# A fused attention and feed-forward block on Trainium2: the rotary feature chain written back into PSUM, and the weight sums emitted one operation per slot

## The chip, the cores and the metric

The kernel runs on one core of one Trainium2 chip. What counts is the device time of one execution in microseconds. The core has five engines that the text names as the profile does: PE (TensorE, matrix products; PEld is its weight load), DVE (VectorE), ACT (ScalarE), POOL (GpSimd) and SP, whose queue issues all DMAs here. SBUF is the working memory; PSUM, eight banks of 128 partitions by 512 float32, receives matrix products.

## The reference

One sequence of 4096 tokens of width 512 passes through linear attention with 16 query heads and 4 key/value heads of 128, and then through a feed-forward block whose weights are surrounded by Hadamard transforms; each is followed by a residual sum and a layer norm. All is float32. Cut to the part that the change touches:

```python
q = q * cos + _rotate_half(q) * sin
k = k * cos + _rotate_half(k) * sin
qf = jax.nn.elu(q) + 1.0
kf = jax.nn.elu(k) + 1.0
def step(carry, inp):
    state, z = carry
    state = state + k_s[..., :, None] * v_s[..., None, :]
    z = z + k_s
    num = jnp.einsum('bhe,bhed->bhd', q_s, state)
    den = jnp.einsum('bhe,bhe->bh', q_s, z)[..., None] + EPS
    return ((state, z), num / den)
```

The feature is elu(x)+1, which the kernel computes as max(x+1, min(exp(x), 1)) with x+1 kept and exp taken with a bias of -1.

## The kernel before

Float32 precision comes from splitting each operand into a high part of the fast matrix type and a rest (`hilo`, L88 to L90: a copy on ACT at L89, a subtraction on DVE or POOL at L90), and from three products per pair.

The attention runs twice over 16 blocks of 256 tokens (n from 0 to 31), each time with half of the heads. One block has four slots (n, g, p), g a key/value head of the half, p a half of the block's four chunks of 64 tokens. The loop over the slots (L437) emits pieces of several generators, each `yield` being a place where the next piece of another one is put between. Per block there are four query projections (`proj_q`, five slots ahead of their use, QA = 5), one key projection (`proj_k`), one value projection (`proj_v`), the transposed keys (`nat_k`, L282), two states (`state`, L294), and in each slot scores (`scores`, L337 and L338, whose result is copied, corrected and masked at L344 to L351) and the numerators and denominators (`av`, L371 and L372).

Every projection has 24 matrix products into one PSUM bank of the pool pmm (L239, L191), which has three banks that rotate. For q and k the result `ps_qk` then goes through `rope`: ACT copies the two halves crosswise into the SBUF tile sw (L224, L225), POOL multiplies sw with the sine (L226), DVE multiplies ps_qk with the cosine in place (L227), DVE adds both and 1 into a new SBUF tile x1 (L230), ACT takes the exponential of x1 into sw (L231), DVE takes min and max (L234): for q into sw itself, for k into the feature tile kft. `proj_q` splits the feature afterwards: a copy into qh (L323) and the rest into ql (L325). The last reader of the PSUM bank is L230.

`wcomb(p)` (L385), for p from 0 to 7, makes sums of the feed-forward weights for later: it loads four tiles of 256 KB from wug, makes four sums on POOL (L394) and stores each by DMA. The tiles come from wres, the pool of 28 tiles that also holds the split attention weights. It is called whole in the slot (1,0) of the blocks n from 18 to 25 (L500). The second half of the attention weights is loaded from block 13 on, and the first reciprocals of denominators (`recip`) follow from block 17.

The order in which the instructions finally stand on each engine is made by the framework's scheduler: it keeps the dependences, estimates durations, and places each instruction by these and by the order of emission. Semaphores are set accordingly, and each engine runs its own order strictly.

After the attention come the output projection with the first layer norm (L724), the feed-forward's first product (L848) and its second (L971).

Of the kernel before, what the change touches and what calls it, by code (L numbers as in the profile page):

```python
# [9 lines left out]
F32 = mybir.dt.float32  # L10
F32R = mybir.dt.float32r
I32 = mybir.dt.int32
AF = mybir.ActivationFunctionType
ALU = mybir.AluOpType
# [29 lines left out]
def kernel(  # L44
# [6 lines left out]
    V, S, G, T = nc.vector, nc.scalar, nc.gpsimd, nc.tensor  # L51

    def dma(dst, src, pin=False):
        if dst.dtype == F32R:
            dst = dst.bitcast(F32)
        if src.dtype == F32R:
            src = src.bitcast(F32)
        i = nc.sync.dma_start(dst, src)  # L58
        if pin:
            tc.keep_in_program_order(i)  # L60

    cpool = ctx.enter_context(tc.tile_pool(name="cpool", bufs=1))
    wres = ctx.enter_context(tc.tile_pool(name="wres", bufs=28))
# [76 lines left out]
    with ExitStack() as es:  # L140
        early = ExitStack()
        pe = early.enter_context(tc.tile_pool(name="ae", bufs=2, side="right"))
# [11 lines left out]
        neg1 = p1.tile([128, 1], F32, name="neg1")  # L154
# [4 lines left out]
        def weights_v(s, j):  # L159
            W["v", s, j] = load_w(wv[s, :, j * 512:(j + 1) * 512])  # L160

        def weights_k(s, g):
            W["k", s, g] = load_w(wk[2 * s + g])

        def weights_q(s, g):
            for h in range(4):
                W["q", s, g, h] = load_w(wq[8 * s + 4 * g + h])
# [52 lines left out]
        def rope(ps, csb, f):  # L220
            cosb = csb[:, 0:1].to_broadcast([128, 2, 256])
            sinb = csb[:, 1:2].to_broadcast([128, 2, 256])
            sw = pe.tile([128, 2, 256], F32, tag="sw", name="sw", bufs=3)
            S.activation(sw[0:64], ps[64:128], AF.Copy)  # L224
            S.activation(sw[64:128], ps[0:64], AF.Copy)  # L225
            G.tensor_tensor(sw, sw, sinb, ALU.mult)  # L226
            V.tensor_tensor(ps, ps, cosb, ALU.mult)  # L227
            yield
            x1 = pe.tile([128, 2, 256], F32, tag="x1", name="x1", bufs=3)
            V.scalar_tensor_tensor(x1, ps, 1.0, sw, ALU.add, ALU.add)  # L230
            S.activation(sw, x1, AF.Exp, bias=neg1)  # L231
            yield
            f = sw if f is None else f
            V.scalar_tensor_tensor(f, sw, 1.0, x1, ALU.min, ALU.max)  # L234
            return f

        def proj(n, keys):
# [89 lines left out]
        def scores(j):  # L327
            n, g, p = slots[j]
            B = blk[n]
            qh, ql = B["q", g]  # L330
            pool, tag = (pmm, "mm") if j >= NQ - TAIL and j % 2 else (psc, "sc")
            ps = pool.tile([128, 2, 256], F32, tag=tag, name="ps_sc")
            for c2 in range(2):
                c = 2 * p + c2
                t = slice(64 * c, 64 * c + 64)
                khl = B["khl"][:, g, c]
                T.matmul(ps[:, c2], khl.rearrange("p l j -> p (l j)"), qh[:, :, t], start=True, stop=True)  # L337
                T.matmul(ps[0:64, c2], khl[:, 0], ql[:, :, t], start=False, stop=True,  # L338
                         skip_group_check=True)
            am = p2.tile([64, 512], F32, tag="am", name="am")  # L340
            A = p3.tile([128, 2, 256], F32R, tag="A", name="A", bufs=4)
            Af = A.rearrange("p a b -> p (a b)")
            psf = ps.rearrange("p a b -> p (a b)")
            S.activation(Af[0:64], psf[0:64], AF.Copy)  # L344
            B["A", g, p] = A
            yield
            V.tensor_tensor(am, psf[0:64], Af[0:64].bitcast(F32), ALU.subtract)  # L347
            V.tensor_tensor(Af[64:128], psf[64:128], am, ALU.add)
            for h in range(2):
                ah = Af[64 * h:64 * h + 64].rearrange("p (a q) -> p a q", q=64)  # L350
                G.affine_select(ah, ah.bitcast(F32), pattern=[[0, 8], [1, 64]], compare_op=ALU.is_ge,  # L351
                                fill=0.0, base=0, channel_multiplier=-1)
# [32 lines left out]
        def wcomb(p):  # L385
            r = {}
            for it in range(2):
                for kh in range(2):
                    x = wres.tile([128, 2, 2, 128], F32, tag="w", name="wq")
                    dma(x, wug[2 * p + it].rearrange("p (u k m) -> p u k m", u=2, k=4)[:, :, 2 * kh:2 * kh + 2])  # L390
                    r[it, kh] = x
            for key, o, a, b, op in (("S3", (0, 0), (0, 0), (1, 0), ALU.subtract), ("S1", (1, 0), (1, 0), (1, 1), ALU.add),
                                     ("S2", (1, 1), (0, 0), (1, 1), ALU.subtract), ("S4", (0, 1), (0, 1), (1, 1), ALU.add)):
                G.tensor_tensor(r[o], r[a], r[b], op)  # L394
                dma(was_d[p][key], r[o].rearrange("p u k m -> p (u k m)"))

        N = 2 * NB
# [14 lines left out]
        def go(gen):  # L412
            if gen is not None:
                next(gen, None)

        def run(gen):
            for _ in gen:
                pass
# [14 lines left out]
        for j in range(SA):  # L433
            run(scores(j))
        nsc = SA
        gk = gs1 = gv = None
        for i, (n, g, p) in enumerate(slots):  # L437
            nxt = n + 1 < N
            sl = (g, p)
            r = i - 4 * (NB - 1)  # L440
            if r == -6:
                for j in range(2):
                    weights_v(1, j)
                    weights_k(1, j)
            if r == 1 - QA:
                weights_q(1, 0)
            if r == 3 - QA:
                weights_q(1, 1)
            if i == NQ - 10:
                load_wo(NH - 2)  # L450
            if i == NQ - 3:
                early.close()
                late["s"] = ExitStack()
                late["p"] = late["s"].enter_context(tc.tile_pool(name="cl", bufs=2, side="right", reuse_waits="tile"))
                pre(0)
            go(gq)
            if sl == (0, 1):
                go(gk)
            if sl == (1, 0):
                go(gk)  # L460
            gq2 = proj_q(i + QA) if i + QA < NQ else None
            go(gq2)
            if sl == (0, 0):
                gk = proj_k(n + 1) if nxt else None
                go(gk)
                go(gs1)
                gs2 = state(n, 1)
                go(gs2)
            elif sl == (0, 1):
                gv = proj_v(n + 1) if nxt else None  # L470
                go(gv)
                go(gk)
                if n + 2 < N:
                    run(load_x(n + 2))
            elif sl == (1, 0):
                if nxt:
                    nat_k(n + 1)
            else:
                gs1 = state(n + 1, 0) if nxt else None
                go(gs1)  # L480
            go(gq)
            gsc = []
            while nsc < NQ and nsc <= i + SA + (i >= NQ - TAIL) + (i > NQ - TAIL):
                gsc.append(scores(nsc))
                go(gsc[-1])
                nsc += 1
            go(gq)
            if sl == (0, 0):
                go(gs2)
            elif sl == (0, 1):  # L490
                go(gv)
            elif sl == (1, 1):
                go(gs1)
            av(n, g, p)
            if sl == (0, 0):
                go(gs2)
            for x in gsc:
                go(x)
            gq = gq2
            if sl == (1, 0) and 18 <= n < 26:  # L500
                wcomb(n - 18)
            if sl == (1, 1):
                if NB + LAG <= n < N - 2 + LAG:
                    recip(n - NB - LAG)
                blk.pop(n - 1, None)
# [15 lines left out]
    def xtile(shape, dt, name):  # L521
        return mid.tile(list(shape), dt, tag="x4", name=name, bufs=2)
# [101 lines left out]
    with ExitStack() as es:  # L624
# [19 lines left out]
        for h in (NH - 2, NH - 1):  # L644
            w = xtile([128, 2, 512], F32R, "wx")
# [68 lines left out]
        for t in range(32):  # L714
            if t + 2 < 32:
                pre(t + 2)
            ps = pwo.tile([128, DM], F32, tag="wo", name="ps_wo")
# [35 lines left out]
            if t >= 29 and t < 31:  # L753
                x = late["p"].tile([128, 16, 128], F32, tag="nt", name="araw0", bufs=2)
                x = x.rearrange("p (s u k) m -> p s u k m", s=4, u=2)
# [41 lines left out]
    with ExitStack() as es:  # L797
# [23 lines left out]
        for n in range(NS):  # L821
            f, p = divmod(n, 8)
# [14 lines left out]
            for s, tag in enumerate(SEQ):  # L837
# [3 lines left out]
                for u in (1, 0):  # L841
                    if first:
                        bank[tag, u] = pgu.tile([128, 512], F32, tag=tag, name="ps_" + tag, bufs=4 if tag == "a" else 2)
                    ps = bank[tag, u]
# [8 lines left out]
                    if s in (0, 2, 4):  # L853
                        x = pa.tile([128, 512], F32, tag="sv", name="sv", bufs=6)
                        S.activation(x, ps, AF.Copy, scale=sc)  # L855
                        sv[s, u] = x
                    if s in (1, 4, 6):
                        src, k, q = {1: (ps, 0, 0), 4: (bank.get(("b", u)), 4, 3), 6: (ps, 2, 1)}[s]
                        x = utile("cc")
                        V.scalar_tensor_tensor(x, src, sc, sv[k, u], ALU.mult, ALU.add)  # L860
                        emit(u, q, x)
                    if s == 5:
                        if u == 1:
                            x = utile("sg")
                            S.activation(x, ps, AF.Silu, scale=sc)
                            c["g", 2] = x
                        else:
                            x = c.pop(("g", 2))
# [44 lines left out]
    with ExitStack() as es:  # L913
# [34 lines left out]
        for idx, (n, s) in enumerate(order):  # L948
# [10 lines left out]
            tag = SEQ[s]  # L959
# [3 lines left out]
            ps = bank[n, tag]  # L963
# [86 lines left out]
```

## Time and profile before

| what | us |
|---|---|
| three timed runs: median | 2352.28 |
| three timed runs: lowest and highest | 2348.13, 2353.02 |
| the profiled execution | 2347.88 |
| its span, first to last instruction | 2345.7 |
| busy PE, PEld | 2270.4, 2014.8 |
| busy DVE, ACT, POOL | 1808.5, 1403.3, 1244.4 |

The span of the profiled execution is the sum over all stages; the attention takes the first 966 us of it. Busy time on PE counts modelled ends of pipelined matrix products, so a full PE shows no holes, but isn't shown to be at its peak. In the groups of instructions the last columns say how long the engine idled just before them and what ended the idleness. A wait is put down to the semaphore that came last. The granted clock of PE was 0.988 of full speed over the span.

### The profile page before, as it was taken

How to read it: one execution, taken by the hardware profiler on the slowest of the kernel's cores; microseconds unless marked ns; L12 is line 12 of the kernel's file. 1: busy time of each engine (PE TensorE's matmuls, PEld its weight loads, DVE VectorE, ACT ScalarE, POOL GpSimd, SP SyncE). 2: the span in 40 equal slices, each digit the busy share in tenths (PEclk: the TensorE clock that was granted, in tenths of full speed). 3: DMA queues.
4: the chain of work that ended last, by engine and by line, in shares of the span. 5: the costliest groups of instructions: out<-in, count | busy, mean ns of one | idle time of the engine just before them, and what ended most of it. 6: DMA issues, size and time to landing. Idle time of an engine off the chain costs nothing.

```text
span 2345.7 us, 42356 instructions
## 1 busy us (share of the span) xinstructions
PE 2270.4 (97%) x14432; PEld 2014.8 (86%) x14432; DVE 1808.5 (77%) x2799; ACT 1403.3 (60%) x2482; POOL 1244.4 (53%) x1000
## 2 busy tenths in 40 slices
PE   7999999998999999799999999999999999899998
PEld 6999999988899999688878777788878888799998
DVE  6999999988798889778898676686776766765554
ACT  5777777766677777444444466655655655555553
POOL 2454544576654445367888526565565556633332
PEclk9999999999999999899999999999999999999999
DMA  6454555677744444878997977786666766877673
GB/s 185 145 147 147 157 159 151 177 213 219 209 133 133 129 132 139 276 253 266 283 294 257 303 238 217 237 256 188 226 208 189 243 189 198 278 238 249 224 253 117
DMA packets 369528, 484.16 MB, mean 206 GB/s; under 512 B 68670, under 2 KB 224384, under 8 KB 365344
## 3 DMA queue, kind: packets, MB, share of 16 engines
q1 hardware_dynamic: 369312, 481.45, 66.4%
q8 instruction: 114, 1.87, 0.3%
q14 instruction: 102, 0.84, 0.1%
HBM read 282.76 MB, written 156.76 MB: 187 GB/s over the span
## 4 chain that ended last, share of the span: by engine, by line
PE 78%; DVE 8%; DMA 6%; issue 4%; POOL 2%; ACT 2%; SPq 1%; DVEq 0%; ACTq 0%; POOLq 0%
PE ps_a L848 14%; PE ps_qk L244 13%; PE ps_wo L724 12%; PE ps_da L971 8%; PE ps_b L848 7%; PE ps_num L371 5%; PE ps_db L971 4%; PE ps_c L848 3%; PE ps_s L294 3%; PE ps_v L197 3%; PE ps_dc L971 2%; PE ps_sc L337 1%; PE ps_den L372 1%; PE ps_sc L338 1%; SPq L58 1%
## 5 line engine op out<-in xcount | busy, mean ns | idle before, releaser
L351 POOL TENSOR_SCALAR_AFFINE_SELECT A<-A 64x512 fp32r<-64x512 f32 x256 | 219.1, 856 | 289.5 <-DVE am L347 185.7
L244 PE MATMUL ps_qk<-xh,wh 128*128 128x256 f32 x1280 | 359.8, 281 | 7.6 <-ACT wh L89 3.9
L244 PE MATMUL ps_qk<-xh,wl 128*128 128x256 f32 x1280 | 358.1, 280 | 0.0
L244 PE MATMUL ps_qk<-xl,wh 128*128 128x256 f32 x1280 | 358.0, 280 | 0.0
L90 DVE TENSOR_TENSOR wol<-A,woh 128x512 fp32r<-128x512 f32 x217 | 229.1, 1060 | 112.4 <-ACT woh L89 94.6
L830 POOL TENSOR_TENSOR cc<-cc 128x512 f32<-128x512 f32 x96 | 148.7, 1550 | 286.1 <-ACT cc L827 137.2
L226 POOL TENSOR_TENSOR sw<-sw,csb 128x512 f32<-128x512 f32 x160 | 219.9, 1375 | 143.3 <-ACT sw L225 135.2
L244 PEld LDWEIGHTS ps_qk<-xh,wh 128*128 128x128 f32 x1280 | 243.5, 190 | 9.2 <-ACT wh L89 4.1
L244 PEld LDWEIGHTS ps_qk<-xl,wh 128*128 128x128 f32 x1280 | 242.9, 190 | 1.3
L244 PEld LDWEIGHTS ps_qk<-xh,wl 128*128 128x128 f32 x1280 | 242.9, 190 | 0.8
L89 ACT ACTIVATE hah<-hraw 128x512 fp32r<-128x512 f32 x224 | 139.8, 630 | 133.5 <-PE ps_da L971 64.3
L89 ACT ACTIVATE woh<-A 128x512 fp32r<-128x512 f32 x217 | 135.6, 630 | 131.1 <-PE ps_b L848 74.9
L90 POOL TENSOR_TENSOR hal<-hraw,hah 128x512 fp32r<-128x512 f32 x80 | 105.8, 1324 | 189.9 <-PE ps_da L971 66.1
L848 PE MATMUL ps_a<-yoh,woh 128*128 128x512 f32 x512 | 202.4, 397 | 1.8 <-ACT sv L855 1.4
L848 PE MATMUL ps_a<-yol,woh 128*128 128x512 f32 x512 | 202.5, 396 | 0.0
L848 PE MATMUL ps_a<-yoh,wol 128*128 128x512 f32 x512 | 199.3, 396 | 0.0
L90 DVE TENSOR_TENSOR hal<-hraw,hah 128x512 fp32r<-128x512 f32 x144 | 106.2, 746 | 117.0 <-PE ps_da L971 41.8
L724 PE MATMUL ps_wo<-wh,oh 128*128 128x512 f32 x448 | 178.6, 399 | 4.6 <-ACT oh L89 4.6
L724 PE MATMUL ps_wo<-wh,ol 128*128 128x512 f32 x448 | 178.3, 398 | 0.0
L724 PE MATMUL ps_wo<-wl,oh 128*128 128x512 f32 x448 | 177.9, 397 | 0.0
L231 ACT ACTIVATE sw<-x,neg 128x512 f32<-128x512 f32 x160 | 115.5, 722 | 79.9 <-DVE x L230 78.0
L855 ACT ACTIVATE sv<-ps_a,wsc 128x512 f32<-128x512 f32 x192 | 127.1, 679 | 40.0 <-PE ps_a L848 39.9
(215 smaller groups left out, 7273.8 us busy)
## 6 DMA issues: line engine op xcount, KB each, us to landing
hraw<-hop_d SPq DMA_DIRECT2D x224, 256.0 KB
vd<-vhl SPq DMA_DIRECT2D x128, 256.0 KB
num_d<-num SPq DMA_DIRECT2D x128, 256.0 KB
rb<-rec_d SPq DMA_DIRECT2D x128, 256.0 KB
hop_d<-hS SPq DMA_DIRECT2D x128, 256.0 KB
nt<-num_d SPq DMA_DIRECT2D x31, 1024.0 KB
A<-in_wug_dram SPq DMA_DIRECT2D x93, 256.0 KB
hop_d<-cc SPq DMA_DIRECT2D x64, 256.0 KB
```

Source lines behind the costliest of these rows:

```text
L89: S.activation(hi, src, AF.Copy)
L90: eng.tensor_tensor(lo, src, hi.bitcast(F32), ALU.subtract)
L226: G.tensor_tensor(sw, sw, sinb, ALU.mult)
L231: S.activation(sw, x1, AF.Exp, bias=neg1)
L244: T.matmul(ps[:, j], W[key][wa][:, k * 128:(k + 1) * 128], B[xa][:, k], start=i == 0, stop=i == 11)
L351: G.affine_select(ah, ah.bitcast(F32), pattern=[[0, 8], [1, 64]], compare_op=ALU.is_ge, fill=0.0, base=0, channel_multiplier=-1)
L371: T.matmul(ps[:, c2], l, r, start=i == 0, stop=i == len(ops) - 1)
L724: T.matmul(ps, l[:, h], r, start=i == 0, stop=i == 47)
L830: G.tensor_tensor(x, x, c.pop(("g", q)), ALU.mult)
L848: T.matmul(ps, w[:, u, k], y[:, k], start=first and i == 0, stop=i == 5, skip_group_check=not first)
L855: S.activation(x, ps, AF.Copy, scale=sc)
L971: T.matmul(ps[:, j], ops[qd][al][:, r, js], BW[s][bl][ip], start=first and i == 0, stop=i >= 45, skip_group_check=True)
```

## The change

Two edits, both in the attention.

In `rope` the tile x1 is gone. The sum of L230 is written into ps_qk in place, the exponential reads ps_qk, and the minimum and maximum for q are written into ps_qk, too, in place of sw; for k they go into kft as before. `proj_q` is not edited, but its feature f is now the PSUM tile, so the copy into qh and the subtraction into ql read PSUM. So the bank is held until ql is made (q) or until kft is written (k).

`wcomb` becomes a generator that yields after its four loads and after each sum (the store of a sum is emitted at the next step), and `wcomb_all` runs the eight of them one after another. One step is emitted per slot in the blocks 17 to 27: 44 steps, of which 41 have work. The tiles get another name; pool and tag stay.

```diff
-            x1 = pe.tile([128, 2, 256], F32, tag="x1", name="x1", bufs=3)
-            V.scalar_tensor_tensor(x1, ps, 1.0, sw, ALU.add, ALU.add)
-            S.activation(sw, x1, AF.Exp, bias=neg1)
-            yield
-            f = sw if f is None else f
-            V.scalar_tensor_tensor(f, sw, 1.0, x1, ALU.min, ALU.max)
+            V.scalar_tensor_tensor(ps, ps, 1.0, sw, ALU.add, ALU.add)
+            S.activation(sw, ps, AF.Exp, bias=neg1)
+            yield
+            f = ps if f is None else f
+            V.scalar_tensor_tensor(f, sw, 1.0, ps, ALU.min, ALU.max)
             return f
@@
-                    x = wres.tile([128, 2, 2, 128], F32, tag="w", name="wq")
+                    x = wres.tile([128, 2, 2, 128], F32, tag="w", name="wsum")
                     dma(x, wug[2 * p + it].rearrange("p (u k m) -> p u k m", u=2, k=4)[:, :, 2 * kh:2 * kh + 2])
                     r[it, kh] = x
+            yield
             for key, o, a, b, op in (("S3", (0, 0), (0, 0), (1, 0), ALU.subtract), ("S1", (1, 0), (1, 0), (1, 1), ALU.add),
                                      ("S2", (1, 1), (0, 0), (1, 1), ALU.subtract), ("S4", (0, 1), (0, 1), (1, 1), ALU.add)):
                 G.tensor_tensor(r[o], r[a], r[b], op)
+                yield
                 dma(was_d[p][key], r[o].rearrange("p u k m -> p (u k m)"))
@@
+        def wcomb_all():
+            for p in range(8):
+                yield from wcomb(p)
+
+        gw = wcomb_all()
@@
-            if sl == (1, 0) and 18 <= n < 26:
-                wcomb(n - 18)
+            if 17 <= n < 28:
+                go(gw)
```

## The prediction

> **What bounds the kernel now.** I read the busy table, then the busy time by stage, then the chain of waits inside each stage, then the groups of the chain that the change edits, then the waits of the one stage in which TensorE is not full. The edited code runs only in the attention stage, about 0 to 966 us. By stage (length, then busy time of PE, PEld, DVE, ACT, POOL, then granted clock):
>
> ```profile
> 60.00:400.00 340.00, 339.90 (x2770) 324.14 (x2770) 315.63 (x521) 258.30 (x464) 169.12 (x156) 1.00 0.52 151
> 400.00:700.00 300.00, 279.32 (x2182) 261.81 (x2180) 259.91 (x417) 200.62 (x358) 180.34 (x161) 0.98 0.66 191
> 700.00:930.00 230.00, 230.00 (x1876) 219.50 (x1876) 202.12 (x346) 170.72 (x301) 110.77 (x110) 1.00 0.47 131
> 930.00:980.00 50.00, 36.06 (x211) 29.99 (x210) 37.42 (x60) 25.87 (x49) 21.50 (x24) 0.83 0.75 226
> ```
>
> In 60 to 400 and 700 to 930, 570 us, TensorE has no hole. A busy PE need not be at its peak, so I looked at matmul starts: 0.114 us apart in L244, almost without exception, and the same run of 38 matmuls recurs at 723.73, 751.67, 779.61 us, so a token block takes 27.94 us. The chain in those windows is nearly all PE. VectorE, 88 to 93% busy, is second and not on the end. The holes are elsewhere: in 0 to 60 (weights arriving, then VectorE), in 400 to 700 (second weight half, weight sums, first reciprocals) and in the drain after 930. Adding what each matmul start is late against its usual spacing, PE loses about 30 us in 400 to 660, 25 of them in 18 gaps over 0.5 us.
>
> The groups that the change edits (count | busy us, mean ns | idle before):
>
> ```profile
> L325 DVE TENSOR_TENSOR ql<-sw,qh 128x512 fp32r<-128x512 f32 x128 | 126.3, 987 | 6.8 <-ACT qh L323 5.6
> L231 ACT ACTIVATE sw<-x,neg 128x512 f32<-128x512 f32 x160 | 115.5, 722 | 79.9 <-DVE x L230 78.0
> L227 DVE TENSOR_TENSOR ps_qk<-ps_qk,csb 128x512 f32<-128x512 f32 x160 | 110.9, 693 | 25.6 <-ACT sw L225 24.2
> L230 DVE SCALAR_TENSOR_TENSOR x<-ps_qk,sw 128x512 f32<-128x512 f32 x160 | 108.6, 679 | 29.8 <-POOL sw L226 29.4
> L234 DVE SCALAR_TENSOR_TENSOR sw<-sw,x 128x512 f32<-128x512 f32 x128 | 92.4, 722 | 3.3 <-ACT sw L231 2.2
> L234 DVE SCALAR_TENSOR_TENSOR kft<-sw,x 128x512 f32<-128x512 f32 x32 | 30.8, 963 | 0.4 <-ACT sw L231 0.4
> ```
>
> L227 and L230, with one input in PSUM, hold 672 to 700 and 669 to 693 ns over all 160; L325 and L234, with both inputs in SBUF, spread to 2069 and 2405 ns. The waits of 440 to 700 us (total, times, longest):
>
> ```profile
> POOL wq L394 <- DMA wq<-in_wug_dram: 15.2, 7, 5.0
> PEld ps_num L371 <- POOL A L351: 13.2, 12, 3.4
> PE ps_num L371 <- POOL A L351: 10.5, 9, 3.2
> POOL wq L394 <- issue: 8.3, 2, 5.2
> PE ps_sc L337 <- DVE A L348: 6.1, 5, 2.2
> PEld ps_qk L244 <- DVE x L230: 2.5, 2, 1.6
> ```
>
> A weight sum whose load is late blocks POOL, the mask (L351) behind it is late, and PE waits for it. A projection waits for its bank (last row) almost never.
>
> **What the Trainium skill says.** "SBUF — State Buffer", section "Who interferes with whom": a VectorE instruction with at most one SBUF input doesn't contend with GpSimd, one with two contends with GpSimd reads. The spreads above agree. "PSUM — Partial Sum Buffer", section "Specifications (TRN2)": VectorE may take one tensor input from PSUM, GpSimd none. The new operations keep to it, and POOL's multiply L226 stays as it is. "Perfetto Trace Analysis", section "Optimization Strategy": equal bubbles on the engine that should be full can mean too few buffers; before, those two windows show none. No page prices a bank held longer.
>
> **The change, part by part.**
>
> *Faster VectorE operations.* Both inputs in SBUF become one. Taking 690 ns (L227's and L230's level): L325 128 x (987-690) = 38.0 us; L234 into the feature tile 128 x (722-690) = 4.1; L234 into kft 32 x (963-690) = 8.7; L230 now writes PSUM, as L227 does: 160 x (693-679) = +2.2. Together -48.6 us of VectorE. ScalarE reads PSUM in L231 and L323: copies from PSUM take 588 (L201), from SBUF 631 ns (L323), so -43 ns x 288 = -12 us. In the 570 us with PE full this is hidden behind PE and worth nothing. In 400 to 700 the pieces of the chain add up to some 81 us DVE, 53 DMA, 28 issue, 25 POOL, the rest mostly PE. VectorE's saving there is about a third of 48.6, 16 of 260 us or 6%, so 81 x 6% = 5 us. POOL, less disturbed (L226 means 1434 ns there, 1301 in the quiet window): 6% of 25, 1.5 us. Fill, where 21 of 30 us to 60 are DVE on the chain: 6%, 1.5 us with rounding. Drain: 0. ACT: 0. Sum -8; bounds 0 (DMA decides anyway) and -20 (most holes of the 30 us close, since a VectorE that is less loaded catches up sooner).
>
> *The bank is held longer.* The three banks of pmm rotate: projection j+3 takes the bank of j. Now the last reader is L230; after it is the subtraction into ql (for k the write of kft). Following each tile through the trace by the built order: from first matmul to the end of L230 9.5 us mean in 60 to 400 (8.2 in 700 to 925), to the end of L325 14.3 (13.5). The third next projection starts 14.0 us after a tile on average (two of them are one block: 27.94). Before, 4.5 to 5.8 us are spare. After, the built order keeps tiles more together (26.7 matmuls from a tile's first to last, formerly 30.3: -0.4 us), and VectorE work from L227 to ql falls from 7.9 to 7.4 us (-0.5), so the hold is about 12.6 to 13.4 and the spare 0.6 to 1.4.
>
> The tightest link in the built order is the q tile before k, whose bank the v projection takes. Ahead of its ql VectorE has k's add, sl and A. From k's last matmul: swaps 1.24, POOL 1.44, add 0.72, sl 0.68, A 0.71, ql 0.70, with waits between about 5.6 to 6.2 us. PE meanwhile has 24 matmuls of 0.114, some 26 of 0.118 and three state ones, 6.3 us. So it just fits, with no cover left: where it doesn't, each missing 0.1 us costs 0.1 us in each of some 20 quiet blocks. I take 0 there, bounds 0 and +8 (0.4 us a block). In 400 to 700 the hold to L325 is 17.5 us in the mean while blocks take about 32 (16 for three tiles): minus 1.4 as above, nothing is spare, and a late POOL operation now delays the bank as well as the mask. Much of that overlaps with waits that PE has anyway: +2, bounds 0 and +16. Behind a waiting projection stand the next scores and numerators in PE's queue, which restart POOL and VectorE: so a missed bank echoes once round. Fill: +1 for the same reason (five q tiles are projected ahead), bounds 0 and +5.
>
> *Weight sums one per slot.* Same 32 sums of 1.26 to 1.75 us, same 32 loads and 32 stores on SP, emitted from block 17 to 27. But the scheduler puts an operation where it thinks the operands are ready: sums stand in the built POOL order behind 82, 83, 84, 84, 85, 85, 85, 86 rope multiplies, formerly 82, 83, 84, 84, 85, 85, 86, 86, and the last behind 105 in both. Freed weight tiles pace them, not the new yields. So the 25 us that POOL idles before L394 mostly stay; another draw of places: -2, bounds -8 and +6. On SP a store that waits for its sum is queued ahead of later loads, as before.
>
> *Freed tile x1*: three SBUF buffers, used by nothing else.
>
> *Sum*: -8 + 0 + 2 + 1 - 2 = -7 us. The profiled execution took 2347.9 us (span 2345.7 and 2.2 around), so 2341 on its own scale. The three timed runs have median 2352.28, 4.4 above it; against these 2345.
>
> **Rivals.** *A, as summed*, 2345, own range 2337 to 2350. *B, the banks decide*: PE waits for a bank in each block, 0.4 x 20 = 8 us, and in 400 to 700 the bank turns POOL's delays into PE holes, +16; fill +5; against -8 and half of -2: +20, 2372; a milder form at half these prices +6, 2358. It decides once the mean hold passes 14.0 us. For it: a spare near 1 us and the link that just fits; in the built order 147 projection rows wait for VectorE alone, formerly 46. Against: a wait in the order isn't a wait in time, and the tiles' own chain, some 9.5 us without queues, leaves 4.5 us for queueing. *C, nothing moves*: PE is full where the operations got cheaper, DMA decides in the holes, the scheduler undoes the spreading: 2352. For it: 570 of 966 us. *D, the holes close*: VectorE and POOL recover before PE notices, 20 of the 30 us gone and 5 of the fill: 2327. For it: L348, L325 and L234 recur on the chain after each DMA delay. Against: 53 us of DMA on the chain are untouched.
>
> **How the numbers follow.** Chances: A 0.42, B 0.34, C 0.13, D 0.11. A measurement here can tell about 0.2%, 4.7 us, from no change. A lies mostly beyond it: 0.36 of 0.42; with D faster gets 0.47. Same: 0.06 of A, C's 0.10, some of mild B: 0.19. Slower: 0.34. The likeliest is 2345. The range takes D nearly whole and B to its full price less a little: 2324 to 2370.
>
> **What would show it.** Right: L324 and L233 at about 690 ns without spread, VectorE some 49 us less busy, PE as full in 60 to 400 and 700 to 930 with a 27.94 us block, fewer PE waits for A in 400 to 700. Wrong through B: waits of ps_qk and ps_v for VectorE's ql in each block, a block over 28.2 us, a lower granted clock. Wrong through D: PE's holes after 400 halved. If the sums alone matter, POOL's waits for wsum loads vanish while the bank waits stay nil.

## The result, and the profile after

The change made the kernel no faster: 2351.39 us after it (median of 12 runs, 2347.04 to 2354.41) beside 2347.94 before it on the same chip (median of 12, 2344.77 to 2353.02), a ratio of 1.0009 with a 95% interval of 1.0001 to 1.0017. The forecast was a gain of 7 us. The profiled execution after the change took 2354.41 us with a span of 2352.5, that of before 2347.88 with 2345.7. The former is the slowest of its twelve runs, 3 us above their median, so the stages below overstate the difference by about that much.

The edited operations did what was foreseen for them. The groups of instructions after the change (count | busy us, mean ns | idle time before, and what ended it):

```profile
L324 DVE TENSOR_TENSOR ql<-ps_qk,qh 128x512 fp32r<-128x512 f32 x128 | 88.0, 687 | 18.5 <-ACT qh L322 16.6
L233 DVE SCALAR_TENSOR_TENSOR ps_qk<-sw,ps_qk 128x512 f32<-128x512 f32 x128 | 88.1, 688 | 2.5 <-ACT sw L230 1.1
L233 DVE SCALAR_TENSOR_TENSOR kft<-sw,ps_qk 128x512 f32<-128x512 f32 x32 | 21.7, 678 | 0.2
L230 ACT ACTIVATE sw<-ps_qk,neg 128x512 f32<-128x512 f32 x160 | 109.9, 687 | 56.1 <-DVE ps_qk L229 54.7
L226 POOL TENSOR_TENSOR sw<-sw,csb 128x512 f32<-128x512 f32 x160 | 209.0, 1307 | 187.6 <-ACT sw L225 174.0 <-POOL A L350 8.7 <-issue 1.3
L350 POOL TENSOR_SCALAR_AFFINE_SELECT A<-A 64x512 fp32r<-64x512 f32 x256 | 197.9, 773 | 282.2 <-DVE am L346 179.9 <-DVE A L347 97.7 <-PE ps_qk L243 0.7
```

The two groups of GpSimd before it, the multiply and the causal mask:

```profile
L226 POOL TENSOR_TENSOR sw<-sw,csb 128x512 f32<-128x512 f32 x160 | 219.9, 1375 | 143.3 <-ACT sw L225 135.2 <-POOL A L351 1.5 <-DVE A L348 0.8
L351 POOL TENSOR_SCALAR_AFFINE_SELECT A<-A 64x512 fp32r<-64x512 f32 x256 | 219.1, 856 | 289.5 <-DVE am L347 185.7 <-DVE A L348 69.3 <-DVE khl L272 26.0
```

The rest ql fell from 987 to 687 ns, the key's minimum and maximum from 963 to 678, and GpSimd's multiply and mask, which nobody edited, from 1375 to 1307 and from 856 to 773. VectorE's idle time before ql rose from 6.8 to 18.5 us: it finished earlier and waited more. The same stages as before (length, then busy PE, PEld, DVE, ACT, POOL, then granted clock):

```profile
60.00:400.00 340.00, 340.00 (x2761) 322.69 (x2760) 303.17 (x519) 253.61 (x462) 150.34 (x156) 1.00 0.54 151
400.00:700.00 300.00, 280.01 (x2153) 262.04 (x2153) 239.66 (x409) 195.70 (x354) 161.98 (x159) 0.96 0.63 186
700.00:930.00 230.00, 228.54 (x1840) 214.74 (x1838) 188.03 (x340) 160.87 (x293) 105.91 (x107) 1.00 0.49 132
```

Read the counts of matmuls, not the busy time: with more or less full PE there are 2761 in place of 2770 in 60 to 400, 2153 in place of 2182 in 400 to 700, and 1840 in place of 1876 in 700 to 930. PE does less in each of these stretches although VectorE is freer in each. (The stretches are fixed, so a kernel that starts its blocks later also shows fewer matmuls.) The granted clock of PE in 400 to 700 us, the last column but two, is 0.96 after the change, 0.98 before. The waits of the two full stages, one fence for each (60 to 400, then 700 to 930; total, times, longest), show a line that before was not there:

```profile
PEld ps_v L197 <- DVE ql L324: 2.3, 11, 0.2
```

```profile
PEld ps_sc L336 <- DVE A L347: 2.5, 6, 0.5
PEld ps_v L197 <- DVE ql L324: 1.9, 8, 0.2
```

Eleven and eight times, about once in each block, the value projection waits for the bank that ql releases. In the fill a query projection waits 4.9 us for ql. So the bank is felt. The waits put down to ql are small, but they aren't all that PE stands still: the second full stage has 2.5 us for the correction A of the scores beside them.

A sharper measure is the start of each block's key transposes, which every kernel has 32 times. In us:

| kernel | block 2 starts | 2 to 12 | 12 to 22 | 22 to 30 |
|---|---|---|---|---|
| before | 94.3 | 278.7 | 312.8 | 223.5 |
| after | 98.1 | 281.2 | 316.5 | 227.8 |

After the change 3.8 us are lost in the fill, 2.5 in the first full stage, 3.7 in the stage with the weight work, 4.3 in the second full stage. In the two full stages the listed waits have the size of the loss: 2.3 us in the first, and 2.5 and 1.9 in the second. The drain gives 6.4 of these 14.2 back: the output projection starts at 978.8 in place of 971.0.

### The profile page after: what moved, and what is told of

It reads as the page before. It is cut to its first block, busy times and chain, and to the rows that moved or that the text cites. A ratio compares the mean times of both kernels' runs of the same rounds, so it can differ in the third digit from the quotient of the medians.

```text
span 2352.5 us, 42271 instructions
## 1 busy us (share of the span) xinstructions
PE 2280.3 (97%) x14432; PEld 2018.4 (86%) x14432; DVE 1768.2 (75%) x2799; ACT 1390.4 (59%) x2482; POOL 1208.7 (51%) x1000
## 4 chain that ended last, share of the span: by engine, by line
PE 79%; DMA 8%; DVE 6%; POOL 2%; issue 2%; ACT 2%; SPq 1%; ACTq 0%; DVEq 0%; POOLq 0%
PE ps_wo L731 14%; PE ps_a L855 13%; PE ps_qk L243 13%; PE ps_da L978 8%; PE ps_b L855 7%; PE ps_num L370 5%; PE ps_db L978 4%; PE ps_v L197 3%; PE ps_c L855 3%; PE ps_s L293 3%; PE ps_dc L978 2%; PE ps_sc L336 1%; DMA den_d<-ds 1%; DMA wsum<-in_wug_dram 1%; PE ps_den L371 1%
## 5 line engine op out<-in xcount | busy, mean ns | idle before, releaser
L350 POOL TENSOR_SCALAR_AFFINE_SELECT A<-A 64x512 fp32r<-64x512 f32 x256 | 197.9, 773 | 282.2 <-DVE am L346 179.9
L226 POOL TENSOR_TENSOR sw<-sw,csb 128x512 f32<-128x512 f32 x160 | 209.0, 1307 | 187.6 <-ACT sw L225 174.0
L230 ACT ACTIVATE sw<-ps_qk,neg 128x512 f32<-128x512 f32 x160 | 109.9, 687 | 56.1 <-DVE ps_qk L229 54.7
```

The lines of the kernel that those rows point to most:

```text
L230: S.activation(sw, ps, AF.Exp, bias=neg1)
```

## The experiments

All were timed in five rounds against the kernel before on the same chip. The brackets behind a ratio hold its 95% interval. Differences in us are of medians. The cuts of code leave out unchanged lines.

### Each edit alone

The first kernel has the feature chain in PSUM and the weight sums as before, the second the sums one per slot and the chain as before: each is one of the two edits of the diff shown above.

> Only the feature chain in PSUM; the weight sums as before. Holding theory (the v projection waits for the bank that the q tile before k keeps until ql): the quiet blocks 2 to 12 last 28.1 to 28.2 us as in the changed kernel, formerly 27.87, PEld of ps_v waits for ql in most of them, and the time is that of the changed kernel within 3 us (0 to 6 above before). Sums theory (the sums' new places cost, holding is free): blocks of 27.9 us and a time 4 to 8 us below before. Redraw theory (any edit shifts the schedule by a few us): blocks either way, time anywhere within 6 us.

> Only the weight sums one operation per slot; x1 in SBUF as before. Holding theory: quiet blocks 27.9 us, no bank wait, time within 3 us of before. Sums theory: 3 to 6 us above before, the loss between blocks 15 and 21. Redraw theory: up to 6 us either way between blocks 15 and 21 and nothing elsewhere.

The chain alone took 2353.60 us, ratio 1.0026 (1.0018 to 1.0035), the sums alone 2347.75, ratio 1.0002 (0.9994 to 1.0010). With the sums alone the blocks are as before except from 16 to 21, which shift by up to 3 us each way. So the sums alone are worth nothing that can be measured, and the loss belongs to the chain. With it come the 4.96 us gap between two matmuls of PE in the fill and the 19 waits of the value projection in the full stages. On top of the chain the sums may be worth something: the change with both edits has the ratio 1.0009 (1.0001 to 1.0017), the chain alone 1.0026, some 4 us more, with intervals that don't overlap. The profiled executions, 2354.41 and 2353.54 us, don't show where.

### The bank held longer, the operations as before

```diff
+        late1 = p1.tile([128, 1], F32, name="late1")
@@
             V.tensor_tensor(ql, f, qh.bitcast(F32), ALU.subtract)
+            V.tensor_tensor(late1, ps[:, 0, 0:1], ql[:, 0, 0:1].bitcast(F32), ALU.add)
```

> The kernel before, with one added element operation on VectorE behind each ql that reads ps_qk, so that the bank is held as long as in the change, without the cheaper VectorE operations (128 added operations of about 0.1 us, 13 us of VectorE). Holding theory: the hold is 14.3 us where the third next tile starts 14.0 after, so the bank is short in every block: 0.5 to 2 us a block, 15 to 45 us in all. If holding is free: 0 to 5 us.

2352.92 us, ratio 1.0025 (1.0016 to 1.0035): 6 us, far less than expected. The fill loses 3.9 us up to block 2, and the full stages have blocks of 28.05 and 28.11 us although no wait for a bank is seen there. The reads add 128 x 152 ns = 19.5 us to VectorE, so even these 6 us aren't the bank's alone. Taken by itself this run says that the hold is cheap. With VectorE's operations still slow it is; the last pair of experiments shows that with quick ones it isn't.

### The order of the key's and a query's projection

The bank that the value projection takes is that of the query projected ahead of the key. If the key is projected first, it takes the key's, which is free earlier.

```diff
+            if sl == (0, 0):
+                gk = proj_k(n + 1) if nxt else None
+                go(gk)
             gq2 = proj_q(i + QA) if i + QA < NQ else None
             go(gq2)
             if sl == (0, 0):
-                gk = proj_k(n + 1) if nxt else None
-                go(gk)
                 go(gs1)
```

> The changed kernel with the k projection of a block emitted ahead of the q projection of the slot (0,0), so that v takes the bank of k, which is free when kft is written, and not of the q tile before k. Holding theory: the wait of ps_v for ql goes, quiet blocks fall from 28.13 to 27.9 us, the time is 5 to 9 us below the changed kernel, 2 to 6 below before. If the block is longer for another reason (PE rows in another order, DMA): blocks stay at 28.1 us and the time within 3 us of the changed kernel.

> The kernel before with k emitted ahead of q, the control of e4. There no projection waits for its bank, so holding theory says nothing is gained: time within 2 us of before. If e4's gain comes from the order alone, this gains 3 to 7 us too.

On top of the change: 2345.94 us, ratio 0.9998 (0.9990 to 1.0006). The value projection's waits for ql are gone (three for the key's kft stand in their place, 1.6 us in all) and the full blocks take 28.0 and 27.9 us in the mean, in place of 28.1 and 28.5. In the kernel before the same order leaves them at 27.9 to 28.0 us, so it isn't the order by itself that shortens them: that link was the cause of the longer blocks. The other expectation fell: in the kernel before, where no such wait exists, the same order gained 8.6 us, 2340.18, ratio 0.9963 (0.9949 to 0.9977), in the stage of 400 to 700 us (308.1 us from block 12 to 22) and the drain. An order of emission is worth some 9 us by itself, which limits what smaller differences between kernels of different order can prove.

### More work on VectorE

```diff
+        more = p1.tile([128, 128], F32, name="more")
@@
             V.tensor_tensor(ql, f, qh.bitcast(F32), ALU.subtract)
+            V.tensor_tensor(more, f[:, 0, 0:128], qh[:, 0, 0:128].bitcast(F32), ALU.subtract)
```

> The kernel before with 128 added VectorE operations of 128x128 with two SBUF inputs behind each ql (about 0.2 to 0.25 us each, some 28 us of VectorE, the reverse of more than half of the relief). If the relief of 48.6 us was worth 8 us, as forecast, the reverse costs 4 to 6 us. If VectorE is off the path everywhere that counts: 0 to 1.5 us and quiet blocks of 27.9 us.

2362.26 us, ratio 1.0054 (1.0041 to 1.0068). The 128 added operations take 490 ns each, 62.7 us, and VectorE is busy 44.9 us longer (1853.4 against 1808.5). They cost 13 us, more than expected, most of it from block 12 to 22 (322.5 us). VectorE's load does reach PE, and in that stage: in 400 to 700 us PE waits 11.2 us for VectorE's A and 7.8 us for GpSimd's mask behind it.

### A fourth bank for the projections

```diff
-        pmm = es.enter_context(tc.tile_pool(name="pmm", bufs=3, space=PSUM))
+        pmm = es.enter_context(tc.tile_pool(name="pmm", bufs=4, space=PSUM))
         psc = es.enter_context(tc.tile_pool(name="psc", bufs=1, space=PSUM))
-        pnum = es.enter_context(tc.tile_pool(name="pnum", bufs=2, space=PSUM))
+        pnum = es.enter_context(tc.tile_pool(name="pnum", bufs=1, space=PSUM))
```

> The changed kernel with four banks for projections and one instead of two for the numerators. Holding theory: ps_qk and ps_v never wait for ql, neither in the quiet blocks nor in the fill; what the numerators lose with one bank is seen in e8. Against e8 it is faster by what the VectorE relief is worth: 8 us by the forecast, 0 to 2 us if it is worth nothing.

> The kernel before with the same four and one banks: the price of one numerator bank alone. ACT's copy of a numerator must be done before the next starts: 0 to 60 us above before. Its difference to e7 is the relief without the longer hold, apart from the order of the instructions and the sums.

> The feature chain alone (weight sums as before) with four banks for the projections and one for the numerators. If the sums of the change are worth nothing, this takes what both edits took with four banks, a ratio to before of 0.9888, within 0.003 (2319 to 2330 us where before is 2348). If the sums carry part of that gain, this one is slower by that part: up to 0.997 if they carry most of it. The chain's worth with a bank to spare is this time less that of the kernel before with four banks (ratio 1.0004).

This is the lowest time of the study: the change with four banks takes 2322.60 us, ratio 0.9888 (0.9874 to 0.9902), a gain of 26 us. The kernel before gains nothing from the same banks: 2349.82, ratio 1.0004 (0.9994 to 1.0014). So the bank is worth something only with the faster chain, and the chain only with the bank. The chain without the edit of the sums has 2325.95, ratio 0.9906 (0.9892 to 0.9919), 3 us above that of both edits. The two intervals overlap a little: again some 4 us for the sums on top of the chain, in the same direction as with three banks, and again not settled.

The stages of the change with four banks, in the same columns:

```profile
60.00:400.00 340.00, 340.00 (x2795) 325.05 (x2793) 300.59 (x531) 259.19 (x469) 147.19 (x159) 1.00 0.54 154
400.00:700.00 300.00, 288.88 (x2313) 273.80 (x2312) 249.85 (x434) 209.04 (x379) 167.68 (x169) 0.99 0.68 197
```

In 400 to 700 us PE starts 2313 matmuls where the change with three banks has 2153 and before has 2182, while VectorE's operations there are as quick as with three banks. From block 12 to 22 it takes 295.8 us in place of 316.5, and the stretches of over 0.5 us from one matmul's start to the next, between 400 and 660 us, sum to 13.6 us in place of 25.1.

Two more with four banks: the hold of the third experiment added to the kernel before, and the key's projection first.

> The kernel before with four banks and the one-element read that holds each query bank until its ql is made. If the longer hold costs time only because three banks are too few, the fourth bank takes that cost away: within 3 us of the kernel before with four banks (ratio 1.000 to 1.002, where three banks with the hold had 1.0025). If the hold costs through the order of instructions or the 128 extra reads on VectorE, the cost stays: ratio 1.0025 or more. The fill (0 to 60 us) should then show no wait of a projection for the held bank over 1 us.

> Both edits of the change, four banks, and the key projection emitted ahead of the query projection of the block's first slot. With three banks the order was worth 0.9998/1.0009, 2.5 us after the change and 9 us before it. If that worth came from the bank that v waits for, it is gone with a fourth bank: ratio 0.988 to 0.990 as without it. If it came from the order in the stage of 400 to 700 us itself, it adds: ratio 0.984 to 0.987.

The hold with four banks still cost 1.0023 (1.0014 to 1.0032), 2352.37 us: what it cost with three was therefore mostly not a shortage of banks, but the added reads or the order. The key first took 2328.94 us, ratio 0.9927 (0.9913 to 0.9940), 6 us more than without it and outside both ranges expected: with the bank to spare, its worth is gone and it does harm.

### The relief without the hold, and then the hold alone

What was open: does the longer hold take back a relief that three banks would have given, or does the relief need a fourth bank anyway? A constant PSUM tile, in the bank taken from the numerators, gives the operations their quick form without holding any bank. The kernel leaves out the maximum with x+1 and the true rest: it is a probe of the time, not a replacement.

```diff
-        pnum = es.enter_context(tc.tile_pool(name="pnum", bufs=2, space=PSUM))
+        pnum = es.enter_context(tc.tile_pool(name="pnum", bufs=1, space=PSUM))
+        pone = es.enter_context(tc.tile_pool(name="pone", bufs=1, space=PSUM))
+        one = pone.tile([128, 2, 256], F32, name="half")
+        V.memset(one, 0.5)
@@
-            V.scalar_tensor_tensor(f, sw, 1.0, x1, ALU.min, ALU.max)
+            V.scalar_tensor_tensor(f, sw, 1.0, one, ALU.min, ALU.max)
@@
-            V.tensor_tensor(ql, f, qh.bitcast(F32), ALU.subtract)
+            V.tensor_tensor(ql, one, qh.bitcast(F32), ALU.subtract)
```

> The kernel before, where the minimum and maximum and the rest ql read a constant PSUM tile (0.5) in place of x1 and of the feature: both operations then have one input in SBUF, as after the change, and no bank is held longer. The bank for the constant is taken from the numerators (one in place of two); three banks for the projections. Left out: the maximum with x+1 and the true rest. Theory (the relief is worth some 27 us and the longer hold takes it back): ratio 0.986 to 0.992. Rival (the relief needs a fourth bank, the hold itself costs little): 0.997 to 1.001. The first theory also expects the time between blocks 12 and 22 to be 295 to 302 us, the rival 310 to 316.

2323.01 us, ratio 0.9897 (0.9884 to 0.9910), with three banks for the projections: as good as the change with four. Two controls for the bank taken from the numerators, and one for the reads of the third experiment (the same read of `f` in place of `ps`):

> The change with three banks for the projections and one for the numerators. Control: the gain with four banks and one should come from the fourth, not from the numerators' order. Expected 1.000 to 1.004; if it is 0.99, the numerators' bank is the cause.

> The kernel before with one bank for the numerators, three for the projections. It is the comparison for the run with the constant tile: 0.999 to 1.003.

> The same 128 one-element reads on VectorE as in the run that held the bank, but of the feature in SBUF: no bank is held. They take 128 x 152 ns = 19.5 us of VectorE; at the 13 us that 28 us more of VectorE work cost, 9 us: ratio 1.004. If this is as slow as the run with the hold (1.0025), the hold before the change costs nothing by itself; if it is 1.000 to 1.001, the hold cost those 6 us.

The change with one bank for the numerators and three for the projections took 2366.84 us, ratio 1.0080 (1.0067 to 1.0093), slower than expected: taking the numerators' second bank isn't the source of the gain, it costs the change 7 thousandths. The kernel before with it took 2338.33, ratio 0.9955 (0.9940 to 0.9970), faster, which was not expected. Against this one the relief is worth 15 us. The reads without a hold failed as a control: 2385.81, ratio 1.0161 (1.0148 to 1.0174), because a read of one element from SBUF takes 410 ns in the mean where that from PSUM takes 152, and makes ql slower, too. (Its expectation counts 28 us of VectorE work for the run with more work on VectorE; over the whole span it was 44.9.) What the hold costs in the kernel before stays unseparated from the reads.

The decisive pair changes single operands of the relief alone. Both kernels leave out the true feature, as that one does. First ql reads the projection's own bank, then the minimum and maximum does so instead:

```diff
-            V.tensor_tensor(ql, one, qh.bitcast(F32), ALU.subtract)
+            V.tensor_tensor(ql, ps, qh.bitcast(F32), ALU.subtract)
```

```diff
-            V.scalar_tensor_tensor(f, sw, 1.0, one, ALU.min, ALU.max)
+            V.scalar_tensor_tensor(f, sw, 1.0, ps, ALU.min, ALU.max)
```

> The run with the relief alone (2323.0 us, ratio 0.9897), where only one operand differs: ql subtracts from the projection's own bank in place of the constant one. The same operations with the same kind of inputs, but the bank is held to ql. Left out as there: the true feature. If the hold takes the relief back, this lies at 1.000 to 1.009 (2347 to 2368 us), with the blocks of 700 to 930 us at 28.1 to 28.4 us in place of 27.75 and blocks 12 to 22 at 312 to 320 us. If what the change loses comes from elsewhere (ScalarE reading PSUM, the sum written into the bank, the data), this stays at 0.988 to 0.992.

> As the run with the relief alone, but the minimum and maximum read the projection's bank in place of the constant, and ql the constant: the bank is held to L233's place, some two operations and 1.5 to 2 us less than to ql, and the key's bank to its feature, too. If each 0.1 us of hold has its price, this lies between 0.993 and 1.003; if the loss begins only where v's projection needs the bank that ql frees, 0.988 to 0.992.

Held to ql: 2359.96 us, ratio 1.0052 (1.0040 to 1.0064). One operand turned 0.9897 into 1.0052, 37 us, and the instruction is the same speed, 686 ns beside 684. Held to the minimum and maximum: 2329.81, ratio 0.9925 (0.9910 to 0.9939), 7 us above the relief alone. So most of the price lies between that operation and ql. This falls between the two ranges expected for it, so it decides less than the first of the pair.

The waits of PE's weight load in 60 to 400 us in the run held to ql (total, times, longest):

```profile
PEld ps_sc L340 <- DVE A L351: 8.5, 11, 0.8
PEld ps_qk L247 <- DVE ql L328: 2.6, 11, 0.2
```

The relief alone has no listed wait there. In each block a query projection waits 0.2 us for ql, and the scores wait 0.8 us for VectorE's correction A. Together they are 1.0 us of the 1.1 by which a block is longer (28.93 us in place of 27.80).

The stages of the relief alone and of the held run:

```profile
60.00:400.00 340.00, 340.00 (x2790) 324.95 (x2788) 303.61 (x533) 262.92 (x468) 148.42 (x159) 1.00 0.54 155
400.00:700.00 300.00, 287.78 (x2298) 270.18 (x2297) 247.11 (x432) 211.31 (x376) 167.50 (x168) 1.00 0.66 195
```

```profile
60.00:400.00 340.00, 333.70 (x2684) 313.81 (x2682) 293.47 (x507) 248.12 (x446) 151.74 (x153) 1.00 0.54 149
400.00:700.00 300.00, 281.93 (x2201) 264.59 (x2202) 243.68 (x418) 203.81 (x364) 163.87 (x160) 0.97 0.63 186
```

2790 matmuls against 2684, and 2298 against 2201, by that one operand. In the full stage from block 2 to 12 it takes 289.5 us in place of 280.2 and from 12 to 22 311.8 in place of 297.5. The shape differs from that of the change: from 22 to 30 this kernel loses 1.1 us in place of the 3 to 5 expected. Where the waits fall depends on the order that the scheduler builds, and even this one operand makes it build another: the 37 us are those of the hold with the order that follows from it.

The kernels that decide, by what they have (ratio, then the start of block 2 and the time from block 12 to 22 in us):

| VectorE operations | bank for projections | kernel | ratio | block 2 | 12 to 22 |
|---|---|---|---|---|---|
| slow | three, short hold | before | 1 | 94.3 | 312.8 |
| slow | three, held to ql | before, hold added | 1.0025 | 98.2 | 313.0 |
| slow | three, short hold, one for numerators | before, control | 0.9955 | 95.4 | 305.9 |
| slow | four | before, four banks | 1.0004 | 88.0 | 321.7 |
| quick | three, short hold, one for numerators | relief alone | 0.9897 | 86.7 | 297.5 |
| quick | four | change, four banks | 0.9888 | 91.3 | 295.8 |
| quick | three, held to ql | the change | 1.0009 | 98.1 | 316.5 |
| quick | three, held to ql, one for numerators | change, control | 1.0080 | 98.2 | 317.5 |
| quick | three, held to ql, one for numerators | relief, ql holds | 1.0052 | 93.9 | 311.8 |
| quick | three, held to the maximum, one for numerators | relief, maximum holds | 0.9925 | 93.4 | 300.2 |

Read down the last column: the kernels with quick operations and a bank that is free in time stand at 296 to 300. With either of the two limits left, or with both, it is 306 to 322.

What PE's time from block 12 to 22 consists of shows how the two limits meet. The table counts, in us, the stretches of over 0.15 us in which PE or its weight load stood idle, overlaps counted once, by what ended them, and beside them how long PE's granted clock was at half of full speed:

| kernel | 12 to 22 | PE idle | for GpSimd's mask | for ql | for the state's copies (sh, sl) | at half clock |
|---|---|---|---|---|---|---|
| before | 312.8 | 26.8 | 14.0 | 0 | 0 | 13.7 |
| change | 316.5 | 26.3 | 7.0 | 4.6 | 8.2 | 23.9 |
| change, four banks | 295.8 | 13.2 | 7.6 | 1.7 | 0 | 6.8 |
| relief alone | 297.5 | 16.8 | 7.0 | 0 | 0 | 0 |
| relief, ql holds | 311.8 | 26.1 | 0.6 | 7.5 | 0 | 17.1 |

The quick operations about halve the waits for the mask, or more; where the bank is held with three banks, other waits fill the room again. Half of the last column is what the clock took. Added to the idle time it gives about the differences of the first column: the change lost 9.5 us more in idle time and 11.9 more to the clock than the relief alone, in a stage 19.0 us longer. Why the clock was lower in some runs isn't shown. Over the whole execution it was 0.985 to 0.991 in the twelve runs of the change, and 0.991 to 0.994 in the four of the relief alone.

## Why the prediction was wrong

**The size of the operations: right.** L324 was put at 690 ns and took 687, L233 688 and 678, ScalarE's exponential 687 in place of 722. The reason given for them, the section "Who interferes with whom" of the Trainium skill's page "SBUF — State Buffer" (at most one SBUF input doesn't contend with GpSimd), agrees with the traces on both sides: VectorE's operations lost their spread, and GpSimd's multiply fell from 1375 to 1307 ns and its mask from 856 to 773.

**What the relief is worth: too small.** The term was 8 us, found as 6% of the VectorE and GpSimd pieces of the chain. Measured with a bank that is free in time it is 15 us (relief alone against its control), 24 (against before) or 27 (change with four banks against before with four). The bound of 20 and the rival "the holes close" nearly had the size. Whether it reached PE through VectorE's own saving or through GpSimd's quicker mask, which the prediction gave 1.5 us, isn't separated; from block 12 to 22 the waits for the mask fell by 7 us. The scaling of chain pieces by the saving missed it, since the chain names only the last of several waits; the orders of the kernels compared differ, so the value is known only between 15 and 27.

**What the longer hold costs: the step that failed.** The part "the bank is held longer" was priced at 0 in the full stages, 2 in 400 to 700 and 1 in the fill. Against the relief alone the change starts block 2 11.4 us later, takes 1.0 more up to block 12, 19.0 more up to 22, 5.8 more up to 30 and 0.4 in the drain: 38 us to the start of the output projection, of which 5 are returned after it. The one-operand pair has 37 us. The change and the relief alone differ in the numerators' banks, too; with one bank in both, the medians of whole executions are 44 us apart; for these two kernels as they stand it is 28. In place of +3 the term is some +30. The fill and the stage of 400 to 700 us lie beyond the upper ends that the text had set (5 and 16), the full stages, 6.8, within theirs (8).

The length of the hold was not the mistake. Followed through the trace by the built order, a query's bank is held 12.65 us in the mean in 60 to 400 us, with a longest of 15.3; the prediction had 12.6 to 13.4.

The largest error is the +2 of 400 to 700 us, measured at some 19. The text saw that nothing was spare there (the holds run to 21.3 us, mean 14.5), but took the price to overlap "with waits that PE has anyway". Of those the relief removes a good part, 10 of 26.8 us. Against the kernel before the overlap is real, 26.3 us idle in place of 26.8; against the relief alone it isn't. So the same waits were counted as gained by the relief and as hiding the hold. The clock, which the text had named as a sign of being wrong, was not priced at all.

In the full stages the text compared a mean with a mean, 12.6 to 13.4 against the 14.0 us to the bank's next use, and priced the link named there as tightest, which "just fits", at nothing. It does not quite fit: it is the 0.2 us wait that the value projection has in each full block. With what follows it the block takes 28.1 and 28.5 us in the mean, in place of 27.9. The key first takes the wait and the lengthening away.

**The form of the sum.** Relief and hold were added as if each had its own price. The table of the kernels reads as a maximum: VectorE and the bank each set about the same pace in 400 to 700 us, and taking one limit away uncovers the other. The hold added to slow operations fits, too: 313.0 us beside 312.8. That is a reading of the orders tried, not a law. That both rivals, "the banks decide" and "the holes close", would hold at once was not foreseen; they cancel to +3.4 us.

**The weight sums: -2, measured as nothing alone**, 1.0002 (0.9994 to 1.0010), and perhaps -4 on top of the chain. GpSimd idled 36.9 us before L394, formerly 27.0: the places were drawn anew, and its idle time came out no better. **The fill: +1, measured 3.8** against before and 11.4 against the relief alone. A wait of 4.9 us for ql is in it.

**Still open.** PE's waits for ql at `ps_qk` (11.5 us) and `ps_v` (12.4 us), with its weight load counted beside it, come to roughly 12 us in the change's trace if counted once, of some 30. The rest stands at waits for other things, above all VectorE's A, sl and ScalarE's sh, and at the lower clock. Why these came late isn't followed. The order may have a part in it: in the built order of the change 180 rows of the query, key and value projections wait for VectorE alone, 80 with four banks, 50 before, 29 with the relief alone (147 and 46 in the prediction are of queries and keys). That counts waits in the order, not time. How the price divides between the bank's own waits and the order was not tried, as the order can't be kept while the bank is changed.

## What to carry to other kernels

To move an intermediate from SBUF into the PSUM bank that the matmuls fill is two edits: here it sped up the vector operations and lengthened the hold of a rotating bank. Compare the hold with the time to the bank's next use for the tightest link in the order, not for the mean, and price a link that just fits as one that misses. Where the bank is short, give it one bank more in the same edit: with it this change gained 26 us, without it nothing. Two effects that act on the same waits can't be priced apart and added. "Evacuate promptly", as the section "Summary: rules for kernel authors" of "PSUM — Partial Sum Buffer" in the Trainium skill says, because the memory is small, holds here for a pool of three banks with a number: one operand that kept the bank until ql, 37 us.

## What the runs showed of the hardware that was not expected

- A one-element read with both inputs in SBUF took 410 ns in the mean on VectorE, the same with one input in PSUM 152 ns (128 of each):

```profile
L327 DVE TENSOR_TENSOR late<-sw,ql 128x1 f32<-128x1 f32 x128 | 52.5, 410 | 0.8
```

```profile
L327 DVE TENSOR_TENSOR late<-ps_qk,ql 128x1 f32<-128x1 f32 x128 | 19.5, 152 | 2.7
```

- A full PE isn't one speed: from block 22 to 30, with no listed wait, a granted clock of 1.00 and the same 228 matmuls, a block took 27.74 us (change, four banks), 27.94 (before) or 28.11 (hold added). Whether the order of the matmuls does it, or stops too short to be listed, isn't shown.
- The granted clock of one stage, 400 to 700 us, was 0.96 (change), 0.98 (before), 0.99 (change, four banks) and 1.00 (relief alone).
- The kernel before gains 8.4 us from one bank less for the numerators, and 8.6 from another order of two projections. Neither was looked for, and why isn't known.
